# Attends of two batches in one TensorE block, in a four-layer graph network on one core

## The chip, the core and the metric

The kernel runs on one core of a Trainium2 chip. Its engines run side by side: TensorE (PE, matrix products into PSUM), VectorE (DVE), ScalarE (ACT), GpSimd (POOL) and SyncE (SP, which issues the DMAs here). The metric is the device time of one execution in microseconds (us), as the median of several runs. All data are float32.

## The reference

128 batches of 128 nodes with 512 features go through four layers with a shared 128 x 128 adjacency `adj`. Each layer ends with a layernorm over a residual sum:

```python
# layer 0: aggregate, project
x = _layernorm(x + einsum('nm,bmd->bnd', adj, x) @ w0 + bias)
# layer 1: attention with additive logits s1 + s2, leaky relu, times the mask, softmax, elu
h = x @ W
e = leaky_relu(s1[:, :, None] + s2[:, None, :], 0.2) * adj
x = _layernorm(x + elu(softmax(e) @ h + beta * h))
# layer 2: with W1 = W2 = adj; the differences cancel down to a maximum
A = adj @ x;  C = adj @ x + b
x = _layernorm(x + max_m relu(A[:, :, None, m] + (C - A)[:, :, :, None]))
# layer 3: attention with 8 heads of 64, masked where adj is 0, then proj and layernorm
q, k, v = split(x @ w_qkv)
o = concat_heads(softmax(q k^T / 8 + mask) @ v) @ w_proj + b_proj
x = _layernorm(x + o + layernorm(o) * gamma + beta)
```

The part that changes is `softmax(...) @ v` of layer 3, called the attend below.

## The kernel before

Two batches form a group (`G = 2`), because the query/key product is done for both at once. The order of instructions on each engine is decided ahead of time, on the host, by a small scheduler. Every piece of work is a generator (a "chain") that asks for an engine with `yield use(engine, work, take, ...)`; `take` names the buffers that it needs. The scheduler picks the request that can start first, urgent ones first among equals, and then the lowest rank.

```python
BUFS = {
    "tr": 3, "mm": 3, "sc": 1,
    "x": 16, "yT": 3, "e": 2, "et": 1, "eT": 2, "ex": 2, "xT": 2, "v": 8, "qkT": 3,
    "pr": 2, "pt": 1, "xt": 2, "prT": 2, "oT": 2, "o": 2,
}
# ...
    def at(self, r):
        engine, _, take, _, _ = r["want"]
        t = max(r["ready"] + (MARGIN if engine == "PE" else 0.0), self.free.get(engine, 0.0))
        return max([t, *(self.slots[name][self.next[name]] for name in take())])

    def run(self):
        while self.requests:
            t, _, _, n = min(
                (self.at(r), r["want"][4], r["rank"], n) for n, r in enumerate(self.requests)
            )
            # ... the engine is busy until t + work; the slots are taken; the chain goes on
```

`tr`, `mm` and `sc` are PSUM banks, the others buffers in SBUF. All instructions of one engine run in the order so found. The helpers and the chains for layer 3:

```python
    def product(lhs, rhs):                    # L195 in the profile
        p = bank([P, D], "mm")
        for k in range(K):                    # 4 matmuls, 128x128 by 128x512
            nc.tensor.matmul(p, lhs(k), rhs(k), start=(k == 0), stop=(k == K - 1))
        return p

    def query_key(gr, c):                     # L442: four of these per group, 8 matmuls each
        yield gr.turned                       # xT of both batches has come back by DMA
        # ... 128x128 by 128x256, then a copy to qkT by ScalarE or VectorE

    def values(i, gr, event): ...             # one product, copied to v by ScalarE

    def batch(i):
        # ... layers 0 and 1: mixed() (L203) and product(), twice
        # layer 2, the "gather":
        nc.tensor.matmul(p, adjT, xb, start=True, stop=True)          # L543
        # ... max, layernorm, 32x32 transposes, DMA out and back as xT (features)

        yield gr.qk
        bs = yield use("PE", 1.1, "sc", late=0.2, urgent=True)
        sc = bank([P, 2, K, P], "sc")
        for c in range(K):
            for j in range(2):                # scores, L572: 64 rows by 128
                nc.tensor.matmul(
                    sc[:, j, c, :], gr.qkT[rws, c, nodes], gr.qkT[rws, K + c, nodes],
                    start=True, stop=True,
                )
        # ... VectorE: mask, max (L579, L586); ScalarE: 8 exps (L590);
        # ... VectorE: 1/sum, multiply, transpose (L596, L597, L600) into pt
        yield use("SP", 0.1, late=2.8)
        to_rows(pt.rearrange("p c h s -> p c (h s)"), scratch)
        give(bt)
        bt = yield use("SP", 0.1, "prT", late=4.0)
        prT = buf([P, Q, H * S], "prT")
        from_rows(prT, scratch)
        prT = prT.rearrange("p a (h s) -> p h a s", h=H)

        yield valued

        ba, bo = yield use("PE", 1.1, lambda: ("tr", "oT"), late=0.2, urgent=True)
        p = bank([P, K, P], "tr")
        for c in range(K):
            for j in range(2):                # the attend, L619: lhsT is 128 x 64
                nc.tensor.matmul(
                    p[j * HD : (j + 1) * HD, c, :],
                    valued.v[:, (2 * c + j) * HD : (2 * c + j + 1) * HD],
                    prT[:, j * K + c], start=True, stop=True,
                )
        give(bt)
        give(valued.slot)
        yield use("ACT", 0.6, urgent=True)
        oT = buf([P, K, P], "oT")
        nc.scalar.copy(oT, p)                 # L628
        give(ba)

        bp = yield use("PE", 3.5, "mm", late=0.2)
        p = product(lambda k: oT[:, k, :], lambda k: wproj_sb[:, k, :])
        # ... o = p + bias (L636), layernorm of o (L161 ... L648), layernorm, DMA to out
```

The ranks, where `g` is the group and `i` the batch:

```python
plan.start(query_key(groups[g], n // 2 * 2 + K * (n % 2)), g * G + n / K - (16 if g * G >= NB - 4 else 0))
# ...
plan.start(batch(i), i if i < NB - 4 else i - 16)
```

Of the kernel before, what the change touches and what calls it, by code (L numbers as in the profile page):

```python
# [15 lines left out]
P = 128  # L16
D = 512
K = D // P
G = 2
H = 8  # L20
HD = D // H
# [7 lines left out]
# [5 lines that stand above are left out]
# [9 lines left out]
class Plan:  # L43
# [14 lines left out]
    def use(self, engine, work, take=None, late=0.05, urgent=False):  # L58

        names = take if callable(take) else lambda: (take,) if take else ()  # L60
        return engine, work, names, late, not urgent
# [4 lines left out]
    def done(self, event, late=0.0):  # L66
        event.left -= 1
        event.at = max(event.at, self.now + late)
        if not event.left:
            for r in event.chains:  # L70
                r["ready"] = max(r["ready"], event.at)
                self.step(r, None)

    def give(self, slot):
        name, i = slot
        self.slots[name][i] = self.now
# [13 lines left out]
    def at(self, r):  # L90
        engine, _, take, _, _ = r["want"]
        t = max(r["ready"] + (MARGIN if engine == "PE" else 0.0), self.free.get(engine, 0.0))
        return max([t, *(self.slots[name][self.next[name]] for name in take())])

    def run(self):
        while self.requests:
# [18 lines left out]
def gnn_stack_kernel(  # L115
# [17 lines left out]
    nc = tc.nc  # L133
    NB = x.shape[0]
# [8 lines left out]
    plan = Plan()  # L143
    use, give, done = plan.use, plan.give, plan.done

    def buf(shape, name):
        return work.tile(shape, F32, name=name, bufs=BUFS[name])

    def bank(shape, name):
        return ps.tile(shape, F32, name=name, bufs=BUFS[name])  # L150
# [197 lines left out]
    class Group:  # L348


        def __init__(self):
            self.s = small.tile([P, G, 2], F32, name="s")
            self.logits = [Event(2) for _ in range(G // 2)]
            self.attention = [Event() for _ in range(G // 2)]
            self.turned, self.qk = Event(G), Event(K)
            self.eT, self.xT, self.qkT, self.slot, self.left = {}, None, None, {}, {}

        def read(self, name, of):
# [5 lines left out]
    groups = {}  # L364

    def group(g):
        if g not in groups:
            groups[g] = Group()
            for h in range(G // 2):
                plan.start(attention1(groups[g], h), g * G + 2 * h - (16 if g * G >= NB - 4 else 0))  # L370
            for n in range(K):
                plan.start(query_key(groups[g], n // 2 * 2 + K * (n % 2)), g * G + n / K - (16 if g * G >= NB - 4 else 0))
        return groups[g]


    def attention1(gr, h):
        yield gr.logits[h]
        yield scalars_in
        s = gr.s
        b0 = yield use("PE", 0.3, "tr", late=0.2, urgent=True)  # L380
        p = bank([P, 2, P], "tr")
        for i in range(2):
            nc.tensor.transpose(p[:, i, :], s[:, 2 * h + i, 1:2].to_broadcast([P, P]), ident)  # L383
        be = yield use("DVE", 2.1, "e", urgent=True)
        z = one.tile([P, 2, P], F32, name="z")
        for i in range(2):
            nc.vector.tensor_scalar(
                z[:, i, :].rearrange("p (c r) -> p c r", c=Q),
                p[:, i, :].rearrange("p (r c) -> p c r", c=Q),
                s[:, 2 * h + i, 0:1], None, op0=ALU.add,  # L390
            )
        give(b0)
        e = buf([P, 2, P], "e")
        nc.vector.scalar_tensor_tensor(e, z, ALPHA, z, op0=ALU.mult, op1=ALU.max)
        nc.vector.tensor_tensor(
            e, e, adj_cols.rearrange("p c r -> p (c r)")[:, None, :].to_broadcast([P, 2, P]),
            op=ALU.mult,
        )
        nmx = small.tile([P, 2], F32, name="nmx")
        nc.vector.tensor_reduce(nmx, e, axis=AX.X, op=ALU.max, negate=True)  # L400
        yield use("ACT", 1.2)
        sums = small.tile([P, 2], F32, name="sums")
        for i in range(2):
            nc.scalar.activation(
                e[:, i, :], e[:, i, :], AF.Exp, bias=nmx[:, i : i + 1],
                accum_out=sums[:, i : i + 1],
            )
        bt = yield use("DVE", 1.5, "et")
        rs = small.tile([P, 2], F32, name="rs")
        nc.vector.reciprocal(rs, sums)  # L410
        et = buf([P, Q, 2, S], "et")
        for i in range(2):

            nc.vector.scalar_tensor_tensor(
                e[:, i, :], e[:, i, :], rs[:, i : i + 1], beta_id, op0=ALU.mult, op1=ALU.add
            )
            nc.vector.transpose(et[:, :, i, :], e[:, i, :].rearrange("p (c r) -> p c r", c=Q))
        give(be)
        scratch = dram.tile([P, Q, 2 * S], F32, name="e_d")
        yield use("SP", 0.1, late=2.0)  # L420
        to_rows(et.rearrange("p c i s -> p c (i s)"), scratch)
        give(bt)
        gr.slot[h] = yield use("SP", 0.1, "eT", late=2.6)
        eT = buf([P, Q, 2 * S], "eT")
        from_rows(eT, scratch)
        gr.eT[h] = eT.rearrange("p a (i s) -> p i a s", i=2)
        done(gr.attention[h])


    def query_key(gr, c):  # L430
        yield gr.turned
        yield w3_in
        got = yield use("PE", 3.5, lambda: ("mm",) if gr.qkT else ("mm", "qkT"), late=0.2)
        if gr.qkT is None:
            bp, gr.slot["qkT"] = got
            gr.qkT = buf([P, 2 * K, G * P], "qkT")
        else:
            bp = got
        p = bank([P, 2, G * P], "mm")
        for j in range(2):  # L440
            for k in range(K):
                nc.tensor.matmul(  # L442
                    p[:, j, :], wqkv_sb[:, k, (c + j) * P : (c + j + 1) * P], gr.xT[:, k, :],
                    start=(k == 0), stop=(k == K - 1),
                )
        gr.read("xT", G + K)
        yield use("ACT" if c < K else "DVE", 0.69, urgent=True)
        dst = gr.qkT[:, c : c + 2, :]
        if c < K:
            nc.scalar.mul(dst, p, HD**-0.5)  # L450
        else:
            nc.vector.tensor_copy(
                dst.rearrange("p j (b c r) -> p (j b) c r", b=G, c=Q),
                p.rearrange("p j (b r c) -> p (j b) c r", b=G, c=Q),
            )
        give(bp)
        done(gr.qk)

    def values(i, gr, event):
        b = i % G  # L460
# [31 lines left out]
    def batch(i):  # L492
        g, b = divmod(i, G)
        h = b // 2
        yield loaded[i]
        gr, xb = group(g), xs[i]


# [6 lines left out]
        p = product(lambda k: yT[:, k, :], lambda k: w0_sb[:, k, :])  # L505
# [21 lines left out]
        p = product(lambda k: yT[:, k, :], lambda k: w1_sb[:, k, :])  # L527
# [14 lines left out]
        p = bank([P, D], "mm")  # L542
# [11 lines left out]
        bt = yield use("DVE", 0.65, "xt")  # L554
# [6 lines left out]
        valued = Event()  # L561
# [4 lines left out]
        bs = yield use("PE", 1.1, "sc", late=0.2, urgent=True)  # L566
        sc = bank([P, 2, K, P], "sc")
        nodes = slice(b * P, (b + 1) * P)
        for c in range(K):
            for j in range(2):  # L570
# [3 lines left out]
                    start=True, stop=True,  # L574
# [23 lines left out]
        bt = yield use("DVE", 1.24, "pt")  # L598
# [9 lines left out]
# [3 lines that stand above are left out]
        prT = prT.rearrange("p a (h s) -> p h a s", h=H)  # L611

        yield valued

        ba, bo = yield use("PE", 1.1, lambda: ("tr", "oT"), late=0.2, urgent=True)
        p = bank([P, K, P], "tr")
        for c in range(K):
            for j in range(2):
                nc.tensor.matmul(  # L619
                    p[j * HD : (j + 1) * HD, c, :],  # L620
                    valued.v[:, (2 * c + j) * HD : (2 * c + j + 1) * HD],
                    prT[:, j * K + c], start=True, stop=True,
                )
        give(bt)
        give(valued.slot)
        yield use("ACT", 0.6, urgent=True)
        oT = buf([P, K, P], "oT")
        nc.scalar.copy(oT, p)  # L628
# [3 lines left out]
        p = product(lambda k: oT[:, k, :], lambda k: wproj_sb[:, k, :])  # L632
        give(bo)
        bo = yield use("DVE", 0.69, "o", urgent=True)
# [20 lines left out]
    with tc.manual_schedule(  # L655
        engines={ENG.PE, ENG.DVE, ENG.Activation, ENG.Pool, ENG.SP}
    ):
        plan.start(loads(), 0)
        plan.start(adjacency(), 0)
        for i in range(NB):  # L660

            plan.start(batch(i), i if i < NB - 4 else i - 16)
        plan.run()


# [25 lines left out]
```

## Time and profile before

| What | Value |
|---|---|
| time, median of 3 runs (lowest to highest) | 3364.07 us (3363.28 to 3366.58) |
| span of the profiled execution | 3366.0 us |
| mean granted TensorE clock | 0.996 |
| attend: matmul records on TensorE (L619) | 2048, busy 140.9 us |
| scores: matmul records on TensorE (L572) | 2048, busy 148.7 us |
| products with 512 columns (L195, three groups) | busy 913.9, 464.4 and 460.9 us |
| query/key (L442) | busy 918.2 us |
| VectorE, ScalarE, GpSimd busy | 2669.9, 1189.7, 923.1 us |
| `prT<-p_d`, issue to landing, median | 3.8 us |

How to read it: "busy" of TensorE is the time in which some matmul is under way. Matmuls overlap their neighbours, so the busy time is no measure of how densely they follow each other; that is read from their starts. Each float32 matmul shows as two records, so 8 matmuls are "x16". A timeline row gives start, length, engine, line, operation, `out<-in` with the program's names, the tile of weights, and the count; in brackets the idle time before it and what ended it. A row's last matmul overlaps the start of the next row.

### The profile page before, as it was taken

How to read it: one execution, taken by the hardware profiler on the slowest of the kernel's cores; microseconds unless marked ns; L12 is line 12 of the kernel's file. 1: busy time of each engine (PE TensorE's matmuls, PEld its weight loads, DVE VectorE, ACT ScalarE, POOL GpSimd, SP SyncE). 2: the span in 40 equal slices, each digit the busy share in tenths (PEclk: the TensorE clock that was granted, in tenths of full speed). 3: DMA queues.
4: the chain of work that ended last, by engine and by line, in shares of the span. 5: the costliest groups of instructions: out<-in, count | busy, mean ns of one | idle time of the engine just before them, and what ended most of it. 6: DMA issues, size and time to landing. Idle time of an engine off the chain costs nothing.

```text
span 3366.0 us, 43501 instructions
## 1 busy us (share of the span) xinstructions
PE 3324.6 (99%) x14729; PEld 2070.5 (62%) x14729; DVE 2669.9 (79%) x5527; ACT 1189.7 (35%) x3457; POOL 923.1 (27%) x1031
## 2 busy tenths in 40 slices
PE   9999999999999999999999999999999999999987
PEld 5665656566565666566656656665656665666655
DVE  7878786886978878877877886887887787788775
ACT  3433333333233334343333333333333333333332
POOL 2322221331322312312322331232232232232221
PEclk9999999999999999999999999999999999999999
DMA  4332323223232323222232322232322323232222
GB/s 157 98 103 63 104 75 93 69 80 113 68 99 76 97 79 91 94 79 82 79 109 66 100 85 91 85 89 83 91 85 82 98 73 97 76 94 88 69 82 75
DMA packets 458191, 296.01 MB, mean 88 GB/s; under 512 B 315888, under 2 KB 389744, under 8 KB 457968
## 3 DMA queue, kind: packets, MB, share of 16 engines
q1 hardware_dynamic: 457968, 293.23, 29.0%
q8 instruction: 117, 1.92, 0.2%
q14 instruction: 106, 0.87, 0.1%
HBM read 150.54 MB, written 142.61 MB: 87 GB/s over the span
## 4 chain that ended last, share of the span: by engine, by line
PE 90%; DVE 6%; DMA 2%; issue 1%; SPq 0%; ACT 0%; POOL 0%; POOLq 0%; DVEq 0%; ACTq 0%
PE mm L195 47%; PE mm L442 27%; PE tr L203 6%; PE sc L572 4%; PE tr L619 4%; PE mm L543 3%; DVE st L161 1%; DMA p_d<-pt 1%; DMA prT<-p_d 1%; DVE scr L516 1%; DVE x L648 1%; PE tr L383 0%; SPq L486 0%; DVE t L645 0%; DVE x L182 0%
## 5 line engine op out<-in xcount | busy, mean ns | idle before, releaser
L442 PE MATMUL mm<-xT,wqkv_sb 128*128 128x256 f32 x4096 | 918.2, 381 | 8.8 <-DVE st L161 8.8
L195 PE MATMUL mm<-w_sb,yT 128*128 128x512 f32 x2048 | 913.9, 596 | 2.3 <-ACT yT L206 2.3
L442 PEld LDWEIGHTS mm<-xT,wqkv_sb 128*128 128x128 f32 x4096 | 771.4, 190 | 138.3 <-issue 20.6
L168 POOL TENSOR_TENSOR rstd<-ve,neghalf 128x1 f32<-128x1 f32 x640 | 406.6, 635 | 1100.6 <-DVE ve L165 996.9
L195 PEld LDWEIGHTS mm<-w_sb,yT 128*128 128x128 f32 x2048 | 383.3, 191 | 453.3 <-issue 441.6
L188 POOL TENSOR_TENSOR x<-x,o 128x512 f32<-128x512 f32 x128 | 175.9, 1374 | 1128.3 <-DVE o L636 1117.6
L195 PE MATMUL mm<-wqkv_sb,xT 128*128 128x512 f32 x1024 | 464.4, 596 | 0.0
L195 PE MATMUL mm<-wproj_sb,oT 128*128 128x512 f32 x1024 | 460.9, 598 | 1.8 <-ACT oT L628 1.8
L590 ACT ACTIVATE pr<-pr,nmx 128x128 f32<-128x128 f32 x1024 | 397.6, 391 | 176.1 <-DVE nmx L586 174.6
L161 DVE BATCH_NORM_STATS2 st<-x 128x6 f32<-128x512 f32 x512 | 348.1, 680 | 3.1 <-ACT x L550 1.9
L579 DVE TENSOR_TENSOR pr<-sc,maskb 128x1024 f32<-128x1024 f32 x128 | 156.3, 1221 | 218.8 <-PE sc L572 218.0
L195 PEld LDWEIGHTS mm<-wproj_sb,oT 128*128 128x128 f32 x1024 | 191.8, 191 | 223.6 <-issue 214.4
L177 ACT ACTIVATE x<-x,nmr,rstd 128x512 f32<-128x512 f32 x256 | 205.0, 810 | 351.6 <-DVE nmr L175 326.9
L195 PEld LDWEIGHTS mm<-wqkv_sb,xT 128*128 128x128 f32 x1024 | 189.6, 190 | 199.0 <-issue 191.4
L206 ACT COPY yT<-tr 128x512 f32<-128x512 f32 x256 | 146.8, 582 | 263.9 <-PE tr L203 263.6
L188 POOL TENSOR_TENSOR x<-x,beta_sb 128x512 f32<-128x512 f32 x128 | 167.1, 1307 | 177.1 <-DVE xt L556 131.2
L516 DVE SCALAR_TENSOR_TENSOR scr<-x,wa_rows 128x512 f32<-128x512 f32 x256 | 200.4, 783 | 15.5 <-ACT x L177 10.2
L468 ACT COPY v<-mm 128x512 f32<-128x512 f32 x128 | 74.9, 585 | 347.7 <-PE mm L195 347.5
L450 ACT ACTIVATE qkT<-mm 128x512 f32<-128x512 f32 x128 | 76.1, 594 | 341.2 <-PE mm L442 341.0
L590 ACT ACTIVATION_READ_ACCUMULATOR pr<-pr,nmx 128x1 f32 x1024 | 193.1, 189 | 0.0
L188 POOL TENSOR_TENSOR x<-x,bias_sb 128x512 f32<-128x512 f32 x128 | 182.6, 1436 | 32.9 <-PE tr L203 22.9
L182 DVE TENSOR_SCALAR x<-x,mv,rstd 128x512 f32<-128x512 f32 x256 | 172.5, 676 | 14.4 <-POOL rstd L168 14.0
(63 smaller groups left out, 3558.6 us busy)
## 6 DMA issues: line engine op xcount, KB each, us to landing
p_d<-pt SPq DMA_DIRECT2D x128, 512.0 KB, 2.6
prT<-p_d SPq DMA_DIRECT2D x128, 512.0 KB, 3.8
x<-in_x SPq DMA_DIRECT2D x128, 256.0 KB, 2.9
x_d<-xt SPq DMA_DIRECT2D x128, 256.0 KB, 2.0
xT<-x_d SPq DMA_DIRECT2D x512, 64.0 KB, 2.5
out<-x SPq DMA_DIRECT2D x128, 256.0 KB, 2.0
e_d<-et SPq DMA_DIRECT2D x64, 128.0 KB, 1.7
eT<-e_d SPq DMA_DIRECT2D x64, 128.0 KB, 2.2
```

The costliest lines, as they stand in the source:

```text
L161: nc.vector.bn_stats(st, src)
L168: nc.gpsimd.tensor_tensor(rstd, ve, neghalf, op=ALU.pow)
L177: nc.scalar.activation(xb, xb, AF.Identity, bias=nmr, scale=rstd)
L182: nc.vector.tensor_scalar(xb, xb, mv[:, 0:1], rstd, op0=ALU.subtract, op1=ALU.mult)
L188: nc.gpsimd.tensor_tensor(dst, dst, other, op=ALU.add)
L195: nc.tensor.matmul(p, lhs(k), rhs(k), start=(k == 0), stop=(k == K - 1))
L203: nc.tensor.matmul(p[:, k, :], xb[:, k * P : (k + 1) * P], nodes, start=True, stop=True)
L206: nc.scalar.copy(yT, p)
L442: nc.tensor.matmul(p[:, j, :], wqkv_sb[:, k, (c + j) * P : (c + j + 1) * P], gr.xT[:, k, :], start=(k == 0), stop=(k == K - 1),)
L516: nc.vector.scalar_tensor_tensor(scr, xb, 1.0, wa_rows[:, j, :], op0=ALU.mult, op1=ALU.mult, accum_out=gr.s[:, b, j : j + 1],)
L579: nc.vector.tensor_tensor(pr, sc.rearrange("p j c m -> p (j c) m"), maskb[:, None, :].to_broadcast([P, H, P]), op=ALU.add,)
L590: nc.scalar.activation(pr[:, j, :], pr[:, j, :], AF.Exp, bias=nmx[:, j : j + 1], accum_out=sums[:, j : j + 1],)
```

## The change

The attend becomes a chain of its own that waits for the rows of several batches. For most groups it takes both batches and issues their matmuls as one block on TensorE; for the group with the highest numbers it is started once for each batch. The block asks for two `tr` banks and two `oT` buffers at once, so the scheduler's `at` now looks at the slot that each request of the same name would get. The batches still do their own copy and projection afterwards. And the batches that rank ahead of their numbers become the last six in place of the last four, by 12 ranks in place of 16. The purpose is that TensorE goes over to the attend's 128 x 64 weights once for two batches.

```diff
     def at(self, r):
         engine, _, take, _, _ = r["want"]
         t = max(r["ready"] + (MARGIN if engine == "PE" else 0.0), self.free.get(engine, 0.0))
-        return max([t, *(self.slots[name][self.next[name]] for name in take())])
+        names = take()
+        for n, name in enumerate(names):
+            i = (self.next[name] + names[:n].count(name)) % BUFS[name]
+            t = max(t, self.slots[name][i])
+        return t
...
-                plan.start(attention1(groups[g], h), g * G + 2 * h - (16 if g * G >= NB - 4 else 0))
+                plan.start(attention1(groups[g], h), g * G + 2 * h - (12 if g * G >= NB - 6 else 0))
             for n in range(K):
-                plan.start(query_key(groups[g], n // 2 * 2 + K * (n % 2)), g * G + n / K - (16 if g * G >= NB - 4 else 0))
+                plan.start(query_key(groups[g], n // 2 * 2 + K * (n % 2)), g * G + n / K - (12 if g * G >= NB - 6 else 0))
+
+            for bs in ((0, 1),) if g * G < NB - G else ((0,), (1,)):
+                plan.start(attend(groups[g], bs), g * G - (12 if g * G >= NB - 6 else 0))
...
+    def attend(gr, bs):
+        for b in bs:
+            yield gr.rows[b]
+        slots = yield use(
+            "PE", 0.25 + 0.9 * len(bs), lambda: ("tr", "oT") * len(bs), late=0.2, urgent=True
+        )
+        for n, b in enumerate(bs):
+            valued, prT, bt = gr.heads.pop(b)
+
+            p = bank([P, K, P], "tr")
+            for c in range(K):
+                for j in range(2):
+                    nc.tensor.matmul(
+                        p[j * HD : (j + 1) * HD, c, :],
+                        valued.v[:, (2 * c + j) * HD : (2 * c + j + 1) * HD],
+                        prT[:, j * K + c], start=True, stop=True,
+                    )
+            give(bt)
+            give(valued.slot)
+            gr.o[b] = p, slots[2 * n], slots[2 * n + 1]
+        for b in bs:
+            done(gr.attended[b])
...
         yield valued
-
-        ba, bo = yield use("PE", 1.1, lambda: ("tr", "oT"), late=0.2, urgent=True)
-        p = bank([P, K, P], "tr")
-        ... (the eight matmuls and the two give() that moved into attend)
+        gr.heads[b] = valued, prT, bt
+        done(gr.rows[b])
+        yield gr.attended[b]
+        p, ba, bo = gr.o.pop(b)
         yield use("ACT", 0.6, urgent=True)
...
-            plan.start(batch(i), i if i < NB - 4 else i - 16)
+            plan.start(batch(i), i if i < NB - 6 else i - 12)
```

More of the change, by code (lines that the diff above doesn't have):

```diff
@@ L355, in __init__ @@
             self.turned, self.qk = Event(G), Event(K)
+            self.rows, self.attended = ([Event() for _ in range(G)] for _ in range(2))
+            self.heads, self.o = {}, {}
             self.eT, self.xT, self.qkT, self.slot, self.left = {}, None, None, {}, {}
@@ L613, in batch @@
         yield valued
-        ba, bo = yield use("PE", 1.1, lambda: ("tr", "oT"), late=0.2, urgent=True)
-        p = bank([P, K, P], "tr")
[L617 to L625, printed above, removed]
+        gr.heads[b] = valued, prT, bt
+        done(gr.rows[b])
+        yield gr.attended[b]
+        p, ba, bo = gr.o.pop(b)
         yield use("ACT", 0.6, urgent=True)
```

## The prediction

> **What bounds the kernel now.** I read the page's busy shares and slices first, then TensorE's waits, then the order of time on TensorE in two stretches.
>
> ```profile
> PE 3324.6 (99%) x14729; PEld 2070.5 (62%) x14729; DVE 2669.9 (79%) x5527; ACT 1189.7 (35%) x3457; POOL 923.1 (27%) x1031
> ...
> PE   9999999999999999999999999999999999999987
> ...
> PEclk9999999999999999999999999999999999999999
> ```
>
> TensorE has work in all slices and falls off only in the last two; VectorE, next, is at 79%. So only two things can shorten the run: fewer or denser TensorE nanoseconds, and less idle time at the two ends. TensorE's waits, as engine, line, what it waited for, total us, times, longest:
>
> ```profile
> PE mm L442 <- DVE st L161: 8.8, 1, 8.8
> PE tr L619 <- DMA prT<-p_d: 7.9, 6, 6.0
> ...
> PE mm L195 <- ACT oT L628: 1.8, 2, 1.0
> ```
>
> Of some 31 us in that list, 8.8, 6.0 and most of 1.8 are single events of the tail. In 3200 us between start and tail TensorE waits for hardly anything. "Busy" hides a cost, though: how densely the matmuls start. The timeline of a middle stretch (start us, length us, then the group):
>
> ```profile
> 1495.76 5.31 PE L195 MATMUL mm<-w_sb,yT 128*128 128x512 f32 x12
> 1501.00 1.10 PE L619 MATMUL tr<-prT,v 128*64 128x128 f32 x16
> 1502.02 1.16 PE L203 MATMUL tr<-adjT,x 128*128 128x128 f32 x8
> 1503.02 1.02 PE L543 MATMUL mm<-x,adjT 128*128 128x512 f32 x2
> 1503.97 1.09 PE L619 MATMUL tr<-prT,v 128*64 128x128 f32 x16
> 1505.00 1.98 PE L543 MATMUL mm<-x,adjT 128*128 128x512 f32 x4
> ```
>
> One f32 matmul leaves two records, so an attend of 8 matmuls is x16. Records with 512 columns start 429 ns apart, with 256 columns 216. The x12 group above takes 5.24 us until the attend starts: 11 x 0.429 is 4.72, so the last one took 0.522, which is 93 ns more than its share. Inside an attend block the starts in the trace go 7, 153, 7, 102, 7, 102, ... and after the last record 203 ns pass before other work starts. Two records start nearly together (the two 64-column halves), then a step of about 102: 109.5 per pair, 0.876 us for 16 records. The block takes 1.024 us (1501.00 to 1502.02; the median of all 128 is 1.024). So a lone attend pays 93 on entry, 51 in its first step and 97 on leaving: 0.241 us each.
>
> [...] An attend's lhsT is 128x64, a product's 128x128, a score's 64x128. [...]the extra 93 and 97 ns appear only where the shape of the weights changes. A change from score to attend[...] costs one such step (202 to 205 ns), not two. [...]after the 5.99 us wait near the end, records of 512 columns start 854 ns apart instead of 429. [...] In the old tail the last batch's exps end at 3332.5 by ScalarE's timeline, but its `rs` (L596) runs at 3335.0, behind another batch's `o` (L636), and its transpose (L600) starts at 3340.5, 4.0 us after its input was ready.
>
> **The change, part by part.** It adds no arithmetic: 1024 attend matmuls before and after.
>
> *Pairing.* In the built program's order the old kernel has 128 attend blocks of 8 matmuls, no two adjacent; 37 of their borders are with a score block. The new one has 64 blocks of 16; 12 borders are with a score block. (The two single attends of the last group stand back to back as well.) So 64 blocks vanish: 64 x 0.241 = 15.4 us saved. Twenty-five shared borders are lost, and each had spared one entry of 93 ns: 25 x 0.093 = 2.3 us given back. Net 13.1 us, all on the bounding engine.
>
> *Buffers and waits.* A pair takes two `tr` banks of 3 and both `oT` buffers at once, and holds the first batch's `prT` and `v` until the second has come. The corrected `at` asks for the free time of each slot, so the order is planned around this. A group of two batches has 3364/64 = 52.6 us of TensorE time; a `prT` lands 3.7 us after its issue. I expect little idling and allow 2 us.
>
> *The tail.* Before, batches 124 to 127 rank at 108 to 111 and 120 to 123 end the kernel. After, 122 to 127 rank at 110 to 115, and the last groups are 118/119 and 120/121. Those are normal pairs: "single ones for the last group" applies to 126/127, which no longer come last. The old tail:
>
> ```profile
> 3262.22 7.03 PE L195 MATMUL mm<-wproj_sb,oT 128*128 128x512 f32 x16
> 3278.04 16.80 PE L442 MATMUL mm<-xT,wqkv_sb 128*128 128x256 f32 x64 [8.79 <-DVE st L161]
> ```
>
> ```profile
> 3348.39 1.98 PE L619 MATMUL tr<-prT,v 128*64 128x128 f32 x16 [5.99 <-DMA prT<-p_d]
> ...
> 3351.09 5.77 PE L195 MATMUL mm<-wproj_sb,oT 128*128 128x512 f32 x8 [0.73 <-ACT oT L628]
> ```
>
> The four batches 120 to 123 finish their gathers at 3262 with only two projections left to cover the way from x to `xT`. Lost there: 8.8 us of waiting, and 16.64 - 64 x 0.216 = 2.8 at half clock. Then at the end 1.0 + 6.0 + 0.7 of waits, 0.9 in the slow attend (1.98 against 1.09) and 2.2 in the slow projection (5.77 against 3.60). Together 22.4 us.
>
> In the new order the last two gathers are followed by two projections (6.9), two attends (1.9), one query/key block (3.5), two projections (6.9), three query/key blocks (10.4), values (3.4) and a score (1.1) before the first query/key that needs them: 34 us. Before, the same way took 16 us. The 8.8 and the 2.8 should go.
>
> For the end I walked the new orders of TensorE, VectorE and ScalarE with the old durations, counting from the score of batch 118 as 0. The score of 121 starts at 24.1. The pair 118/119 attends at 28.6 without a wait (its second `prT` lands by about 25), and their projections end at 37.4. Batch 121: mask and max on VectorE to 27.7; ScalarE's exps to 33.1, because the last five stand behind the two `oT` copies of 118/119; normalise to 34.7; `o` of 118, then transpose to 36.6; DMA out 2.6, DMA back 3.9. So its attend starts at about 43.3, after 5.9 us of idling. Then half clock: the pair takes 3.9 instead of 1.9, and the two projections lose another 1.2. In VectorE's order the last `o` is now followed by a layernorm of the other batch: about 1.5 more after the last matmul. Lost: 5.9 + 2.0 + 1.2 + 1.5 = 10.6 us. Against 22.4 that saves 11.8.
>
> Sum: 3364.1 - 13.1 - 11.8 + 2 = 3341 us, a gain of 0.7%.
>
> **The rivals.**
>
> *Coupling.* The pair must wait for its slower member, and needs twice the banks. From a score to its attend took 18.6 to 25.5 us in the tail, so TensorE could stand idle before each pair, or at `mixed`, which shares `tr`. For it: VectorE at 79%[...]. Against it: the order puts tens of us of other work between second score and attend, and the old kernel, with the same margins, waits almost nowhere. At 0.3 us a pair, 19 us come back and the time is about 3360; at 0.6 us it is 3380.
>
> *The switch is hidden or moves.* [...]a second attend in the block might pay the 51 again, or the waiting for its own `prT` might break the block. Then pairing gives 64 x 0.19 - 2.3 = 10 and the time is about 3344. The starts within a block, steady at 102 after the first step, speak against paying more.
>
> *The tail keeps its loss.* The score and exp of the last two batches now have fewer matmuls between them and the end. If my walk is too kind by one softmax (some 6 us), or the order opens a hole elsewhere among the last groups, only about 5 us come from the tail: 3348. The old tail's last chain took 24.6 us against the 19 I give the new one[...].
>
> *VectorE takes over.* Its instruction counts are unchanged, at 79%; I give this nothing.
>
> **Range and chances.** The pairing term is good to some 3 us (10 to 15), the tail to 6, and new waits in the middle lie between -2 and +12. The errors lean towards longer. 3341, with 3331 to 3356 for 8 in 10. Two per cent would be 67 us: the tail's whole loss and the extra of all 128 attends are 22 + 31, so no gain reaches it, and among the rivals only a heavy coupling could. Faster by over 2%: 0.01; within: 0.98; slower: 0.01.
>
> **What would show it.** L619's successor has groups of x32 that take about 1.90 us to the next start, with steps of 7 and 102 through the middle. No wait of 8.8 us for VectorE's `st` in the last 110 us. One wait for `prT` of about 6 us before the last pair, and half clock after it. TensorE's other waits stay within a few us of before. I am wrong if the waits for `prT`, `tr` or `oT` add up to over 10 us in the middle, if the block's middle shows a second 150 ns step, or if the last slices idle as long as before.

## The result, and the profile after

The changed kernel takes 3337.73 us (median of 4 runs, 3337.14 to 3337.99) against 3365.32 us (3363.28 to 3367.11): a ratio of 0.9918, 95% interval 0.9901 to 0.9935. The prediction was 3341 us, range 3331 to 3356.

The page after: busy shares and slices.

```profile
span 3335.1 us, 43586 instructions
...
PE 3303.4 (99%) x14729; PEld 2069.6 (62%) x14729; DVE 2662.2 (80%) x5527; ACT 1185.1 (36%) x3457; POOL 922.5 (28%) x1031
...
PE   9999999999999999999999999999999999999998
```

The number of matmul records is the same and the shares differ by a point at most. The falling digits at the end are one 8 in place of 8 and 7. The cost of the changes of shape can't be seen in these shares, as before.

TensorE's waits after:

```profile
PE tr L392 <- DVE scr L548: 6.2, 8, 1.2
PE tr L480 <- DMA prT<-p_d: 4.4, 2, 4.1
PE tr L207 <- DMA x<-in_x: 3.3, 2, 2.3
```

The 8.8 us for `st` are gone. One wait of 4.1 us for `prT` (L480 is the attend now) stays. The small transposes of layer 1's logits (L392) wait eight times, 6.2 us in all and at most 1.2 us each; before (L383) they waited four times, 2.7 us in all.

A middle stretch of the timeline after:

```profile
1428.94 1.05 PE L207 MATMUL tr<-eT,x 128*128 128x128 f32 x8
1429.92 1.97 PE L480 MATMUL tr<-prT,v 128*64 128x128 f32 x32
1431.82 3.72 PE L451 MATMUL mm<-xT,wqkv_sb 128*128 128x256 f32 x16
1435.38 7.03 PE L199 MATMUL mm<-wproj_sb,oT 128*128 128x512 f32 x16
```

The pair takes 1.90 us to the next start, where two lone attends took 2 x 1.024. Its individual starts are 7, 153, 7, 103, 6, ... and stay at 102 to 103 through the middle, where the second batch begins; then 203 on leaving. Now the row after it: 16 records with 256 columns should last 16 x 0.216 = 3.46 us, and they last 3.56. The extra 0.104 is in their first step, 320 ns instead of 216. That is a cost I had not counted.

The end of the timeline after:

```profile
3299.91 1.97 PE L480 MATMUL tr<-prT,v 128*64 128x128 f32 x32
3301.90 7.13 PE L199 MATMUL mm<-wproj_sb,oT 128*128 128x512 f32 x16
3309.03 1.09 PE L480 MATMUL tr<-prT,v 128*64 128x128 f32 x16
3314.26 1.97 PE L480 MATMUL tr<-prT,v 128*64 128x128 f32 x16 [4.13 <-DMA prT<-p_d]
3316.16 8.57 PE L199 MATMUL mm<-wproj_sb,oT 128*128 128x512 f32 x16
```

The last pair falls in two: batch 120 attends at 3309.03, TensorE waits inside the block for the rows of 121, and after the wait the records come at half clock (the granted clock is 0.50 from 3312.26 to 3319.09; 1.97 us for the attend of 121 against 1.09, 8.57 for the two projections against 7.13 for the two before).

An account of TensorE's time from the starts of all records, in us. "Changes" is what the steps at an entry to a narrow shape (attend or score), the first step in it, the leaving, and the first step after it take above the steady step of their kind. "Waits" is the rest above the steady steps, half clock included: in the first 60 us, in the middle, and in the 130 us before the last matmul. "After" is from the start of the last matmul record to the end. The last two rows belong to the experiments below.

| kernel | span | changes | waits, start | waits, middle | waits, tail | after |
|---|---|---|---|---|---|---|
| before | 3366.0 | 86.5 | 10.3 | 12.5 | 22.7 | 9.7 |
| changed | 3335.1 | 69.6 | 9.4 | 14.1 | 6.8 | 11.0 |
| pairs, old ranks | 3351.0 | 70.1 | 10.4 | 12.4 | 22.9 | 10.9 |
| singles, new ranks | 3358.1 | 87.1 | 9.8 | 14.1 | 13.1 | 9.8 |

What is left (with 2.6 to 2.7 us before the first matmul) is 3221.6 us before and after: the stream itself did not change. Of the 30.9 us of span, 16.9 come from the changes of shape and 15.9 from the tail's waits; 1.3 are given back after the last matmul and 1.6 in the middle, and 0.8 less are waited at the start. With pairs and the old ranks the middle's waits are what they were before (12.4 against 12.5), so the 1.6 us are not shown to be the pairing's; they come in where the ranks change.

### The profile page after: what moved, and what is told of

The parts are those of the page before. It is cut to its first block, busy times and chain, and to the rows that moved or that the text cites. A ratio compares the mean times of both kernels' runs of the same rounds, so it can differ in the third digit from the quotient of the medians.

```text
span 3335.1 us, 43586 instructions
## 1 busy us (share of the span) xinstructions
PE 3303.4 (99%) x14729; PEld 2069.6 (62%) x14729; DVE 2662.2 (80%) x5527; ACT 1185.1 (36%) x3457; POOL 922.5 (28%) x1031
## 4 chain that ended last, share of the span: by engine, by line
PE 87%; DVE 11%; DMA 1%; issue 1%; SPq 0%; ACT 0%; POOL 0%; POOLq 0%; DVEq 0%
PE mm L199 45%; PE mm L451 25%; PE tr L207 5%; PE sc L604 4%; PE tr L480 3%; PE mm L575 3%; DVE st L165 2%; DVE scr L548 1%; DVE x L186 1%; DVE x L541 1%; DVE mv L167 1%; DVE xt L588 1%; DVE x L672 0%; DVE mx L578 0%; DVE x L567 0%
## 5 line engine op out<-in xcount | busy, mean ns | idle before, releaser
L451 PE MATMUL mm<-xT,wqkv_sb 128*128 128x256 f32 x4096 | 908.0, 380 | 1.0 <-DVE mx L578 1.0
L548 DVE SCALAR_TENSOR_TENSOR scr<-x,wa_rows 128x512 f32<-128x512 f32 x256 | 192.2, 751 | 17.8 <-ACT x L181 11.9
L186 DVE TENSOR_SCALAR x<-x,mv,rstd 128x512 f32<-128x512 f32 x256 | 168.1, 661 | 14.4 <-POOL rstd L172 14.3
```

What stands on the lines that cost most here:

```text
L186: nc.vector.tensor_scalar(xb, xb, mv[:, 0:1], rstd, op0=ALU.subtract, op1=ALU.mult)
L451: nc.tensor.matmul(p[:, j, :], wqkv_sb[:, k, (c + j) * P : (c + j + 1) * P], gr.xT[:, k, :], start=(k == 0), stop=(k == K - 1),)
L548: nc.vector.scalar_tensor_tensor(scr, xb, 1.0, wa_rows[:, j, :], op0=ALU.mult, op1=ALU.mult, accum_out=gr.s[:, b, j : j + 1],)
```

## The experiments

My theory: two gains, of the pairing and of the ranks, from fewer changes of the weights' shape and from a covered tail. The rivals: it is all the one or all the other; the cost lies in the block and not in the change of shape; the pair's claim on buffers costs time in the middle.

### Pairing with the old ranks

```diff
-                plan.start(batch(i), i if i < NB - 6 else i - 12)
+                plan.start(batch(i), i if i < NB - 4 else i - 16)
   (likewise for attention1, query_key and attend: 16 if g * G >= NB - 4)
```

> Pairing alone: attends in pairs as in the new kernel, the ranks of the old one (last four batches ahead by 16). Theory (two separate gains, [...]about 14 us from the tail): 3352 us, a ratio of 0.996; [...](63 blocks of 32 records, 1.90 us each), but the tail still loses some 20 us, now mostly as one wait of 10 to 16 us for the last prT. Rival 1 (the whole gain is the tail's, pairing is hidden): 3365. Rival 2 (the whole gain is pairing's): 3338.

Measured: 3351.34 us (3351.01 to 3352.78), ratio 0.9959 (0.9946 to 0.9971). Both "all" rivals miss it. The table shows why it stands there: the changes fall by 16.4 us, and the tail loses as much as it did (22.9 against 22.7). The losses have moved: the 8.8 us for `st` are gone here too, and the waits view of this run shows others in their place:

```profile
PE tr L480 <- DMA prT<-p_d: 15.0, 2, 10.5
...
PE mm L451 <- DMA xT<-x_d: 2.5, 1, 2.5
```

The last pair can't finish before its second batch's rows have come back, and the old ranks leave two projections ahead of it as cover. In its timeline 10.5 us of waiting stand inside the last pair and 4.5 before it.

### The new ranks with single attends

```diff
-            for bs in ((0, 1),) if g * G < NB - G else ((0,), (1,)):
+            for bs in ((0,), (1,)):
```

> The new ranks alone: the attends run through the new chain, but each batch has its own (127 blocks, one of them double by chance). Theory: 3352 us, ratio 0.996; the wait of 8.8 us for VectorE's st near the end is gone, a wait of 1 to 7 us for the last prT stays, and the attends pay 0.241 us each as before. Rival 1 (all tail): 3338. Rival 2 (all pairing): 3365.

Measured: 3358.55 us (3357.81 to 3361.38), ratio 0.9979 (0.997 to 0.9987). The direction is right, the size is not: 7 us of gain, where I expected 13. The end of its timeline shows the missing part:

```profile
3328.06 1.09 PE L480 MATMUL tr<-prT,v 128*64 128x128 f32 x16 [1.59 <-DMA prT<-p_d]
3329.90 5.40 PE L199 MATMUL mm<-wproj_sb,oT 128*128 128x512 f32 x8 [0.74 <-ACT oT L652]
3340.42 1.97 PE L480 MATMUL tr<-prT,v 128*64 128x128 f32 x16 [5.12 <-DMA prT<-p_d]
3343.12 5.75 PE L199 MATMUL mm<-wproj_sb,oT 128*128 128x512 f32 x8 [0.73 <-ACT oT L652]
```

The waits are as expected (1.6 and 5.1), but the projections of both lone attends are slow: 5.40 and 5.75 us against 3.70 for eight records elsewhere. That is 3.8 us that the expectation does not name, and the middle waits 1.6 us more than before. So the two parts are not independent: alone they take 15.0 and 7.9 us off the span, together 30.9 (in medians 14.3 and 7.1, together 27.6). The ranks are worth 15.9 us to the paired order (3351.0 to 3335.1) and 7.9 to the single one. The two changes of the ranks, six batches for four and 12 for 16, were not tested one by one.

### The single attends at the true end

The last group by number, 126/127, gets the single attends, but with the new ranks it does not come last. Here they go to 120/121.

```diff
-            for bs in ((0, 1),) if g * G < NB - G else ((0,), (1,)):
+            for bs in ((0,), (1,)) if g * G == NB - 8 else ((0, 1),):
```

> The new kernel, but the two single attends go to the group that really ends the kernel (batches 120 and 121) and the group 126/127 becomes a pair. Theory (the last wait of 4.13 us stands inside the last pair, because nothing else may run there): the projection of 120 (3.4 us) fills the wait, half clock does not set in, 0.24 us more for one more block: about 4 us less, 3334. Rival (the chain of softmax and DMA of batch 121 sets the end, whatever TensorE does meanwhile): the attend of 121 starts no earlier, but the projection of 120 no longer follows it, so 3.4 us less even then; only if the single attends disturb the order before would nothing be gained, 3338.

Measured: 3334.1 us (3333.82 to 3335.07), ratio to the kernel before 0.9907 (0.9892 to 0.9922). Its median is 3.6 us under the changed kernel's, and their runs don't overlap (3335.07 at most against 3337.14 at least); the intervals of the two ratios do. This version is the fastest of all here. Its end:

```profile
3309.03 1.09 PE L480 MATMUL tr<-prT,v 128*64 128x128 f32 x16
3310.86 3.70 PE L199 MATMUL mm<-wproj_sb,oT 128*128 128x512 f32 x8 [0.74 <-ACT oT L652]
3314.49 1.09 PE L480 MATMUL tr<-prT,v 128*64 128x128 f32 x16
3316.33 3.70 PE L199 MATMUL mm<-wproj_sb,oT 128*128 128x512 f32 x8 [0.74 <-ACT oT L652]
```

The projection of 120 fills the gap, the attend of 121 starts at 3314.49 (3314.26 before), and nothing runs slow (1.09 us for each attend, 3.70 for each projection). The last matmul record starts 4.7 us earlier, at 3319.4. But the span falls by only 2.7: the stretch after it is 13.0 us in place of 11.0. Most of that is VectorE's order. The addition of the last bias, in the changed kernel and here:

```profile
3325.09 0.68 DVE L660 TENSOR_TENSOR o<-mm,bproj_sb 128x512 f32<-128x512 f32 x1
```

```profile
3321.98 0.68 DVE L660 TENSOR_TENSOR o<-mm,bproj_sb 128x512 f32<-128x512 f32 x1
```

It starts 0.36 us after the last projection's end (3316.16 + 8.57 = 3324.73) in the changed kernel, and 1.95 us after it here (3316.33 + 3.70 = 3320.03), where VectorE is still busy with the layernorm of the batch before. So the start of 121's attend is set by its own chain, as the rival says, and what is won is the projection behind it and the time at half clock.

### An extra matmul, of the other shape and of the same

To measure the change of shape by itself, each of the 128 attends of the changed kernel gets extra work in its middle, whose result the attend then overwrites; first one matmul with 128 x 128 weights, then two with 128 x 64. From the steady steps, 112 ns for a record of the one and 109.5 for a pair of records of the other, I estimate 0.22 us for either.

```diff
             for c in range(K):
+                if c == 2:
+                    nc.tensor.matmul(p[:, 3, :], ident, prT[:, 0], start=True, stop=True)
```

> The new kernel with one extra matmul of 128 x 128 weights in the middle of each of the 128 attends; its result is overwritten by the attend's own. Theory (each change of the weights' shape costs 93 on entry, 51 in the first step, 97 on leaving): 128 x (2 x 0.109 + 0.241) = 59 us more, 3397. Rival (the cost is that of the block's start, or of its semaphores, and not of the change of shape): only the matmul's own 0.218 us, 28 us more, 3366.

```diff
             for c in range(K):
+                if c == 2:
+                    for j in range(2):
+                        nc.tensor.matmul(
+                            p[j * HD : (j + 1) * HD, 3, :], ident[:, j * HD : (j + 1) * HD],
+                            prT[:, 0], start=True, stop=True,
+                        )
```

> The new kernel with two extra matmuls of 64 columns each in the middle of each attend, which together stream for as long as the one extra 128-wide matmul of the run before (0.218 us) but keep the shape of the weights; their result is overwritten. Theory (what the 128-wide one cost beyond its own 0.218 us was the change of shape): 128 x 0.219 = 28 us more than the new kernel, 3366, with no step of 150 or 200 ns in the block's middle. Rival (any foreign matmul in the block costs so much): 72 us more, 3409, as the 128-wide one did.

Measured: 3408.66 us (ratio 1.0128, 1.0114 to 1.0142) with the other shape, 3364.23 us (0.9993, 0.9984 to 1.0002) with the same. The spans are 72.0 and 27.8 us above the changed kernel's 3335.1. The same work, in the same places, differs by 44.2 us, or 0.345 us for each of the 128 detours. So the cost goes with the change of shape, not with the block's start or with foreign work in it. But 72 was more than the 59 I gave it. The timeline of the run with the other shape (L480 is the extra matmul there, L482 the attend):

```profile
1457.69 0.66 PE L482 MATMUL tr<-prT,v 128*64 128x128 f32 x8
1458.28 0.49 PE L480 MATMUL tr<-prT,ident 128*128 128x128 f32 x2
1458.69 1.09 PE L482 MATMUL tr<-prT,v 128*64 128x128 f32 x16
1459.72 0.49 PE L480 MATMUL tr<-prT,ident 128*128 128x128 f32 x2
```

The same place in the run with the same shape (L481 is the extra pair, L486 the attend):

```profile
1440.30 0.66 PE L486 MATMUL tr<-prT,v 128*64 128x128 f32 x8
1440.78 0.39 PE L481 MATMUL tr<-prT,ident 128*64 128x128 f32 x4
1441.00 1.04 PE L486 MATMUL tr<-prT,v 128*64 128x128 f32 x16
```

In the first, the extra matmul takes 0.41 us to the next start, in the second 0.22. The individual starts in the first are 203 (leaving), 213 between the extra matmul's own two records, 205 back, and 153 in the attend's first step. The 213 is the term I lacked: among steady records of this shape it is 112, and the control's extra work takes 109 for each pair of records. So the first step after a return costs another 101 to 104. Above the control's steps (102, 109, 109 and 102) the four are 101 + 104 + 96 + 51 = 352 ns. That is a little more than the 345 by which the spans differ; part of the last pair's detours is hidden in its wait for `prT`, which is 3.7 us in this run and 4.2 in the control.

### More buffers for the pair

```diff
-    "pr": 2, "pt": 1, "xt": 2, "prT": 2, "oT": 2, "o": 2,
+    "pr": 2, "pt": 1, "xt": 2, "prT": 3, "oT": 3, "o": 2,
```

> The new kernel with three oT and three prT buffers in place of two each. Theory (pairs wait for their second batch and for two oT hardly anywhere, as the mid-kernel waits grew by under 2 us): no gain, 3337 to 3340, from small differences in the order alone. Rival (the pair's double claim on buffers costs time in the middle): several us less, 3333 or under.

Measured: 3336.9 us (3336.09 to 3337.03), ratio 0.9909 (0.9895 to 0.9924); span 3335.2 us, 13.6 us of waits in the middle against 14.1. So the claim on `prT` and `oT` costs at most the 0.8 us by which the median is lower, and the middle's waits don't show more. More `tr` banks were not tried.

## Why the prediction was right, and where it was off

**What bounds the kernel** held: TensorE's steady stream is the same 3221.6 us, and nearly all that moved were changes of shape and the ends.

**Pairing** was right in what it spares and mis-sized in one term. "0.241 us each" lacked the 104 ns in the first step after the attend, so a lone attend costs 0.345 us; the two runs with extra matmuls give the same. It stood in the lines I had shown: eight records of 128 columns after an attend (1502.02 to 1503.02) take 1.00 us, not 8 x 0.112 = 0.90; the gathers' four records (1505.00 to 1506.82) 1.82, not 4 x 0.429 = 1.72. For the same reason I now estimate that a border shared with a score spares not 93 ns but 0.197 us: the entry, 93, and the step after leaving, 104. Redone: 64 x 0.345 - 25 x 0.197 = 22.1 - 4.9 = 17.2 us, where the account has 16.9 and the prediction 13.1.

**Buffers and waits**: "I expect little idling and allow 2 us" was right in size: 1.6 us more in the middle, though not shown to come from the pairs. The coupling rival is out for the middle, by the waits and by the run with more buffers. At the very end it is real: the last pair waits inside for its second batch, 10.5 us with the old ranks and 4.1 with the new, and splitting that pair saved 3.6 us.

**The tail** gained 14.6 us (waits and half clock 15.9, less 1.3 after the last matmul), predicted 11.8. The 8.8 us and the half clock behind it went, as worked out. The walk put 121's attend 43.3 us after the score of 118; the trace has 3270.64 and 3314.26, so 43.6. What it missed is that the pair's first half does not wait for the second batch: batch 120 attends at once, which takes 1.1 us off the wait. The projections before it also ended later, at 38.4 (3309.03) and not 37.4. So the wait is 4.1 and not 5.9. Only half of the pair then runs at half clock: the 16 records take 1.97 us, where 1.09 is full speed, so 0.9 is lost and not 2.0; the projections lose 1.4 where 1.2 was given.

**The rivals** on the switch and on the tail both pointed to a longer time; both terms came out larger than I had them, on the same side. So the measured time lies 3.3 us under the predicted one. That it is so near is in part luck. In spans the terms were off by more: 3.8 us of pairing, 2.8 of tail, 0.4 of middle waits and 0.8 at the start, 7.8 together. Of that, 3.3 is that the profiled spans lie 30.9 us apart and the medians 27.6 (the profiled execution of the kernel before took 3367.8 us, 2.5 above its median), and 1.2 that the median before was 3364.1 when I predicted and 3365.3 with the fourth run.

## What to carry to other kernels

Where one engine is 99% busy, read the steps between the starts of its instructions, and at every border read the step before it, the first one inside, the one that leaves and the first one after: a change of the weights' shape cost 0.345 us here there and back (44.2 us over 128 detours), in four places, and only two of them (the first step inside and the leaving) lie between the narrow block's first start and the next block's. So it paid here to gather narrow matmuls into longer blocks, and at the very end of the kernel to split them again, so that other work fills the wait for the last operand. When ranks move work to the end, check that special cases bound to "the last" item still meet the one that runs last.

## What the runs showed of the hardware that I had not expected

After a change of shape not only the first start is late but the next step too, in both kernels: by 101 to 104 ns in `mixed` (213 in place of 112), in query/key (320 in place of 216), in products and gathers (533 in place of 429) and in scores, whose records start in pairs (207 in place of 105 at the second pair); by 51 in the attend (153 in place of 102 at its second pair); and by 50 in the small transposes of the logits (159 in place of 109). Why the next step is late was not tested. Two attends' separate waits for their `prT`, inside one block, cost no step: in 61 of the 64 pairs the step in the middle is 102 or 103 ns.

Half clock did not stand beside the long waits of the tail alone. In the kernel before, the granted clock was 0.50 from 3273.37 to 3283.61, around the end of the 8.79 us of idling up to 3278.04, and from 3345.05 to 3355.29, around the end of the 5.99 us up to 3348.39. But TensorE also idled for 2.31 us up to 635.07, and the granted clock was 0.50 from 634.87 to 638.28. With single attends and the new ranks, waits of 1.59 us before an attend and 0.74 before its projection were followed by the projection of 5.40 us in place of 3.70. Single idle times of 1.21 us (up to 909.90, before) and of 1.23 us (up to 283.87, changed) were not followed by it: the granted clock was 1.00.
